# Cross-attention's last key block read in 64-row instead of 32-row TensorE tiles, with its values stored twice between zeros

## The chip, the cores and the metric

The kernel runs on one core of one Trainium2 chip. The metric is the device time of one execution in microseconds (us), lower is better. The time of the kernel before is the median of three runs.

## The reference

One transformer block in float32, batch 2, 1024 tokens of width 256, 16 heads of width 64: self-attention, cross-attention to a context of 154 tokens of width 192, and a gated feed-forward, each behind a layer norm and each added to its input. The part that matters here is cross-attention:

```python
def _attention(xq, xkv, wq, wk, wv, wo, bo):
    B, S, _ = xq.shape
    T = xkv.shape[1]                       # 154 context tokens
    q = (xq @ wq).reshape(B, S, N_HEADS, D_HEAD)
    k = (xkv @ wk).reshape(B, T, N_HEADS, D_HEAD)
    v = (xkv @ wv).reshape(B, T, N_HEADS, D_HEAD)
    attn = jnp.einsum('bihd,bjhd->bhij', q, k) * D_HEAD ** (-0.5)
    attn = jax.nn.softmax(attn, axis=-1)
    out = jnp.einsum('bhij,bjhd->bihd', attn, v).reshape(B, S, D_ATTN)
    return out @ wo + bo
...
x = _attention(h, cond_emb, ca_wq, ca_wk, ca_wv, ca_wo, ca_bo) + x
```

The change is in the second einsum: the softmax weights times the values of the context.

## The kernel before

Attention works on units: one batch element and one pair of heads, 16 units in all (`units`, `NU`). The whole program is emitted in one order written out by hand: a loop over the self-attention steps `p` (128 of them), then a loop over the cross-attention steps `c` (48, three per unit), then a loop over 64 feed-forward slots `k`, the first of which also hold the last steps of cross-attention. Every engine runs its instructions in that order. `run_work` slips projections, output projections and layer norms of other units between the steps; they lie in the lists `work`, `held`, `side` and `outs`. What a piece leaves to copy out is put on a list of stores and flushed a little later. `later` holds DMA issues, which are given out one or two a step.

In cross-attention step `c`, TensorE makes the scores (`sc`, L653), VectorE takes the row maxima (`neg`, L658), ScalarE the exponentials (L669), VectorE the reciprocals of their sums (L677), GpSimd scales the weights (L680), and VectorE transposes them in blocks of 32 by 32 (L696). After this, the 154 keys stand as five blocks of 32 (`NB`, the last one padded with zeros), with a key on each partition. Each of the four partition quarters `a4` (32 partitions each, `KB`) holds one quarter of the queries of a tile, so each quarter is multiplied separately.

So that the multiplication uses more than 32 rows of the array at once, `cross_regroup` moves the first four key blocks by DMA (`wf<-pT_ca` in the profile, since the target shares the buffer `wf`): two key blocks of a quarter are put one below the other, giving 64 rows (`QG`), in `pTc["pairs"]`. The fifth block (`NB - 1`) is not moved: it is read where the transpose left it, in the ring `pTc["ring"]`, as 32 rows of quarter `a4`.

`cross_values(ui, a2)` (L729) is the multiplication. It runs twice for each unit (`a2` of 0 and 1), 32 times in all. A call takes two quarters (`a2` and `2 + a2`) and two heads, so four products, and does each over `m` of 0, 1 and 2: two pairs of blocks, then the last block. The four products of one `m` use different parts of the array, and the profile shows them starting within a few nanoseconds of each other; each float32 matmul of the program appears as two records, so one call is 24 records. In the rest of the text a group of four records that start together is called a wave: a call is six waves, two for each `m`.

The values `v` are made by `values()`, once per two units (8 times): `pv` is projected from the context (L617), ScalarE copies it to `v` (L626, L627), and DMAs put copies where the other quarters need them. `v` lies in the pool `pt_` under the tag `V`, which has two buffers, shared with self-attention's values and, later, the feed-forward's products; a buffer is 8 KB per partition.

The first `values()` runs in the last self-attention steps (step 124), the second in cross step 5, the others every sixth cross step after (11, 17, and so on up to 41). From the third on, it follows the second `cross_values` call of a unit and the VectorE copies of its sums (`store` at L742).

Of the kernel before, what the change touches and what calls it, by code (L numbers as in the profile page):

```python
# [8 lines left out]
F32 = mybir.dt.float32  # L9
# [4 lines left out]
P = 128  # L14
# [4 lines left out]
def tile_transformer_block(ctx: ExitStack, tc: tile.TileContext, a: dict, out: bass.AP):  # L19
    nc = tc.nc  # L20
# [7 lines left out]
    DH = 64  # L28
# [8 lines left out]
    KB = 32  # L37
    NB = -(-T // KB)
    VC = 2 * P
    HB = 512  # L40
    QG = 2 * KB
    TP = NB * KB
    NM = P // QG
# [15 lines left out]
    pt_ = ctx.enter_context(tc.tile_pool(name="pt", bufs=2))  # L59
# [5 lines left out]
    def mm_tile(name):  # L65
        return ps_m.tile([P, HB], F32, tag="mm", name=name)

    def sum_tile(name):

        return ps_o.tile([P, HB], F32, tag="po", name=name)  # L70
# [19 lines left out]
    row_of, r = {}, 0  # L90
# [9 lines left out]
    for n in names[:2]:  # L100
        k = w[n].shape[0] // P
        nc.scalar.dma_start(
            out=cols[:, row_of[n]:row_of[n] + k], in_=w[n].rearrange("(r p) -> p r", p=P)
# [32 lines left out]
    for n in names[2:]:  # L136
        k = w[n].shape[0] // P
        nc.sync.dma_start(
            out=rows[row_of[n] - n_cols:row_of[n] - n_cols + k, :],
            in_=w[n].rearrange("(r p) -> r p", p=P),  # L140
# [34 lines left out]
    hT, vs, qk, oT = {}, {}, {}, {}  # L175
# [116 lines left out]
    def project_half(dst, name, wt, h, n, mul=None, parts=1):  # L292

        pq = mm_tile(f"p{name}_{n}")
        for i in range(parts):
            own = slice(i * HB // parts, (i + 1) * HB // parts)
            for c in range(NC):
                nc.tensor.matmul(  # L298
                    pq[:, own], lhsT=wt[:, c, :],
                    rhs=h[:, c, n * HB + own.start:n * HB + own.stop],  # L300
                    start=(c == 0), stop=(c == NC - 1),
                )
        if mul is None:

            dk = dst.rearrange("p (h n j) -> p n h j", h=2, j=KB)[:, n * NK // 2:(n + 1) * NK // 2]
            return lambda: nc.scalar.copy(dk, pq.rearrange("p (n h j) -> p n h j", h=2, j=KB))
        return lambda: nc.scalar.activation(dst[:, n * HB:(n + 1) * HB], pq, AF.Copy, scale=mul)
# [283 lines left out]
    def cross_pieces(b, pr):  # L591

        t = {}

        def q(n):
            if n == 0:
                t["q"] = p2.tile([P, S], F32, tag="QT", name=f"q_ca{b}_{pr}")
                t["k"] = p2.tile([P, S], F32, tag="KT", name=f"k_ca{b}_{pr}")
                qk["ca", b, pr] = (t["q"], t["k"])
            return project_half(t["q"], f"q_ca{b}_{pr}", wsl["ca", pr, "q"], hT["ca", b], n, scale)  # L600

        def keys():
            pk = mm_tile(f"pk_ca{b}_{pr}")
            for c in range(2):
                nc.tensor.matmul(
                    pk[:, :T], lhsT=wsl["ca", pr, "k"][:, c, :],
                    rhs=ctxT[:, c, b * TP:b * TP + T], start=(c == 0), stop=(c == 1),
                )
            return lambda: nc.scalar.copy(t["k"][:, :T], pk[:, :T])

        def values():

            v = vs["ca", b, pr // 2] = pt_.tile([P, NM + 1, VC], F32, tag="V", name=f"v_ca{b}_{pr}")
            pv = mm_tile(f"pv_ca{b}_{pr}")
            for n, rows_ in ((0, P), (1, KB)):
                for c in range(2):
                    nc.tensor.matmul(  # L617
                        pv[:rows_, n * VC:(n + 1) * VC],
                        lhsT=ctxT[:, c, b * TP + n * P:b * TP + n * P + rows_],
                        rhs=wsl["ca", pr, "v"][:, c, :], start=(c == 0), stop=(c == 1),  # L620
                    )

            def store():
                for n in range(NM):
                    own = slice(n * QG, (n + 1) * QG)
                    nc.scalar.copy(v[own, n, :], pv[own, :VC])  # L626
                nc.scalar.copy(v[:KB, NM, :], pv[:KB, VC:])  # L627
                later.insert(0, lambda: [
                    nc.sync.dma_start(
                        out=v[(1 - n) * QG:(2 - n) * QG, n, :], in_=v[n * QG:(n + 1) * QG, n, :])  # L630
                    for n in range(NM)
                ])
                later.insert(1, lambda: [
                    nc.sync.dma_start(out=v[a4 * KB:(a4 + 1) * KB, NM, :], in_=v[:KB, NM, :])
                    for a4 in range(1, P // KB)
                ])

            return store

        return [lambda: q(0), lambda: q(1), keys] + ([values] if pr % 2 == 0 else [])  # L640
# [74 lines left out]

    def cross_values(ui, a2):

        b, pr = units[ui]
        v, v0 = vs["ca", b, pr // 2], pr % 2 * P
        if a2 == 0 and pr % HP == 0:  # L720
            oT["ca", b, pr // HP] = pt_.tile([P, HP, S], F32, tag="oT", name=f"o_ca{b}_{pr}")
        quarters = (a2, 2 + a2)
        po = {a4: sum_tile(f"poc_{ui}_{a4}") for a4 in quarters}
        for m in range(NM + 1):
            for a4 in quarters:
                r0, n = (a4 // 2 * QG, QG) if m < NM else (a4 * KB, KB)
                r = slice(r0, r0 + n)
                for j in range(2):
                    nc.tensor.matmul(  # L729
                        po[a4][j * DH:(j + 1) * DH, :NT * KB],  # L730
                        lhsT=v[r, m, v0 + j * DH:v0 + (j + 1) * DH],
                        rhs=pTc["pairs"][r, a2, m, j] if m < NM else
                        pTc["ring"][r, ui % 3, NB - 1, j, :],
                        start=(m == 0), stop=(m == NM),
                        tile_position=(r0, j * DH),
                    )
        dst = oT["ca", b, pr // HP][:, pr % HP, :].rearrange(
            "p (t a q) -> p t a q", a=P // KB, q=KB)

        def store():  # L740
            for a4 in quarters:
                nc.vector.tensor_copy(  # L742
                    dst[:, :, a4, :], po[a4][:, :NT * KB].rearrange("p (t q) -> p t q", q=KB)
                )

        return store
# [24 lines left out]
    def cross_weigh(c):  # L771

        for part in range(2):
            ui, n = divmod(c - len(CG) - 4 - part, len(CG))
            if n == 0 and 0 <= ui < NU:
                run(lambda: cross_values(ui, part))
# [245 lines left out]
```

## Time and profile before

| what | value |
|---|---|
| median of 3 runs | 1167.21 us (1166.22 to 1169.26) |
| the profiled execution's own time | 1166.33 us |
| its span, first to last instruction | 1164.5 us |
| TensorE (PE) busy | 1141.3 us, 98% of the span |
| VectorE (DVE) busy | 828.9 us, 71% |
| GpSimd (POOL) busy | 665.8 us, 57% |
| ScalarE (ACT) busy | 643.3 us, 55% |
| cross-attention's value products (L729), span of time | 766.6 to 988.8 us |

Times are of one execution on the slowest core, which here is the only one. In a row such as `766.57 1.09 PE L729 MATMUL poc<-wf,v_ca 64*64 64x256 f32 x16` the first number is the start in us from the span's begin, the second the length, then come engine, line and operation, what is written and read, the tile of the array that is used (rows*columns), the streamed operand, and how many records were merged into the row. A time in brackets is idle time ahead of it, with what ended it. Ends of matmuls are modelled, so spacings are best read from starts.

Busy time by stretches of the span:

| stretch, us | PE | DVE | ACT | POOL |
|---|---|---|---|---|
| 710 to 740 (30) | 26.71 | 25.91 | 18.32 | 25.25 |
| 740 to 766 (26) | 26.00 | 8.63 | 12.43 | 8.19 |
| 766 to 960 (194) | 192.78 | 119.80 | 117.34 | 96.06 |
| 960 to 990 (30) | 30.00 | 12.91 | 7.19 | 9.65 |
| 990 to 1164 (174) | 170.67 | 42.21 | 35.16 | 9.06 |

### The profile page before, as it was taken

How to read it: one execution, taken by the hardware profiler on the slowest of the kernel's cores; microseconds unless marked ns; L12 is line 12 of the kernel's file. 1: busy time of each engine (PE TensorE's matmuls, PEld its weight loads, DVE VectorE, ACT ScalarE, POOL GpSimd, SP SyncE). 2: the span in 40 equal slices, each digit the busy share in tenths (PEclk: the TensorE clock that was granted, in tenths of full speed). 3: DMA queues.
4: the chain of work that ended last, by engine and by line, in shares of the span. 5: the costliest groups of instructions: out<-in, count | busy, mean ns of one | idle time of the engine just before them, and what ended most of it. 6: DMA issues, size and time to landing. Idle time of an engine off the chain costs nothing.

```text
span 1164.5 us, 31710 instructions
## 1 busy us (share of the span) xinstructions
PE 1141.3 (98%) x11931; PEld 673.2 (58%) x11931; DVE 828.9 (71%) x1170; ACT 643.3 (55%) x2055; POOL 665.8 (57%) x1556
## 2 busy tenths in 40 slices
PE   8999999999999999999999999899999999999998
PEld 5434444545545545545545455565566567888887
DVE  4888998898889889888999899557555664232222
ACT  5666676666666656656666666538655572041111
POOL 1778777876777777677777788626644453030000
PEclk9999999999999999999999999899999999999999
DMA  2311011111101101101111010167444433000000
GB/s 80 98 41 34 12 26 34 21 21 34 21 16 35 21 17 26 26 19 21 25 26 21 18 29 11 42 159 183 115 104 99 99 82 69 7 13 10 19 10 18
DMA packets 87234, 51.21 MB, mean 44 GB/s; under 512 B 30814, under 2 KB 77866, under 8 KB 87082
## 3 DMA queue, kind: packets, MB, share of 16 engines
q1 hardware_dynamic: 83866, 46.57, 17.5%
q10 hardware_dynamic: 3216, 2.62, 0.7%
q8 instruction: 94, 1.54, 0.6%
q14 instruction: 58, 0.48, 0.1%
HBM read 19.52 MB, written 2.10 MB: 19 GB/s over the span
## 4 chain that ended last, share of the span: by engine, by line
PE 82%; ACT 6%; POOL 3%; DVE 3%; DMA 2%; issue 2%; SPq 1%; DVEq 0%; ACTq 0%; POOLq 0%
PE po L428 16%; PE s L381 16%; PE pa L817 10%; PE py_sa L359 5%; PE py_ca L359 5%; PE pq_ca L298 5%; PE pf L840 5%; PE poc L729 4%; ACT p L392 4%; PE pv_sa L314 4%; PE pk_sa L298 3%; PE sc L653 3%; PE pq_sa L298 3%; DMA st<-st 2%; DVE st L541 2%
## 5 line engine op out<-in xcount | busy, mean ns | idle before, releaser
L392 ACT ACTIVATE p<-s,st 128x512 f32<-128x512 f32 x512 | 344.7, 685 | 217.9 <-DVE st L541 206.3
L492 POOL TENSOR_SCALAR p<-p,rd,ee 128x512 f32<-128x512 f32 x512 | 385.6, 767 | 43.7 <-DVE rd L488 42.7
L541 DVE TENSOR_REDUCE st<-s 128x2 f32<-128x1024 f32 x256 | 301.2, 1218 | 43.1 <-PE s L381 34.7
L506 DVE STREAM_TRANSPOSE pT<-p 128x1024 f32<-128x1024 f32 x256 | 302.3, 1218 | 1.7 <-POOL p L492 1.7
L381 PE MATMUL s<-k_sa,q_sa 64*32 64x512 f32 x4096 | 253.4, 596 | 12.5 <-ACT p L392 11.2
L428 PE MATMUL po<-pT,v_sa 64*64 64x256 f32 x4096 | 235.8, 379 | 0.0
L428 PEld LDWEIGHTS po<-pT,v_sa 64*64 64x64 f32 x4096 | 150.4, 133 | 109.1 <-issue 37.0
L680 POOL TENSOR_SCALAR p<-p,rden 128x154 f32<-128x154 f32 x256 | 96.8, 398 | 118.3 <-DVE rden L677 118.1
L669 ACT ACTIVATE p<-sc,neg 128x154 f32<-128x154 f32 x256 | 95.8, 394 | 86.6 <-DVE rden L677 82.9
L381 PEld LDWEIGHTS s<-k_sa,q_sa 64*32 64x32 f32 x4096 | 60.0, 105 | 142.4 <-issue 54.5
L817 PE MATMUL pa<-hT_ln,wf 128*128 128x256 f32 x512 | 121.0, 379 | 0.0
L826 DVE SCALAR_TENSOR_TENSOR u<-pa,cols,gate 128x256 f32<-128x256 f32 x64 | 30.9, 484 | 124.2 <-ACT gate L823 124.2
L823 ACT ACTIVATE gate<-pa,cols 128x256 f32<-128x256 f32 x64 | 30.3, 473 | 152.2 <-PE pa L817 152.2
L817 PEld LDWEIGHTS pa<-hT_ln,wf 128*128 128x128 f32 x512 | 96.8, 190 | 13.7 <-issue 0.8
L392 ACT ACTIVATION_READ_ACCUMULATOR p<-s,st 128x1 f32 x512 | 103.7, 202 | 0.0
L658 DVE TENSOR_REDUCE neg<-sc 128x6 f32<-128x924 f32 (+1 forms) x48 | 48.4, 1009 | 51.1 <-PE sc L653 51.1
L416 POOL TENSOR_TENSOR zz<-ee,st 128x8 f32<-128x8 f32 x128 | 25.9, 202 | 76.8 <-ACT ee L414 76.8
L314 PEld LDWEIGHTS pv_sa<-sa_wv,hT_ln 128*128 128x128 f32 x512 | 59.3, 192 | 16.3 <-issue 13.8
L840 PE MATMUL pf<-wf,u 128*128 128x256 f32 x256 | 65.0, 379 | 0.2 <-DVE u L826 0.2
L298 PE MATMUL pq_ca<-hT_ln,ca_wq 128*128 128x512 f32 x128 | 61.9, 625 | 0.5 <-ACT hT_ln L240 0.5
L314 PE MATMUL pv_sa<-sa_wv,hT_ln 128*128 128x128 f32 x512 | 62.4, 278 | 0.0
L359 PE MATMUL py_ca<-ca_wo,o_ca 128*128 128x256 f32 x256 | 60.8, 384 | 0.3 <-ACT hT_ln L240 0.3
(73 smaller groups left out, 1229.4 us busy)
## 6 DMA issues: line engine op xcount, KB each, us to landing
wf<-pT_ca SPq DMA_DIRECT2D x128, 128.0 KB, 2.4
st<-st SPq DMA_DIRECT2D x512, 1.0 KB, 1.7
v_sa<-v_sa SPq DMA_DIRECT2D x64, 128.0 KB, 2.5
wf<-in_L_xattn_ff_w_dram SPq DMA_DIRECT2D x12, 256.0 KB, 5.8
sa_wq<-in_L_xattn_sa_wq_dram SPq DMA_DIRECT2D x16, 128.0 KB, 2.3
sa_wk<-in_L_xattn_sa_wk_dram SPq DMA_DIRECT2D x16, 128.0 KB, 2.4
sa_wv<-in_L_xattn_sa_wv_dram SPq DMA_DIRECT2D x16, 128.0 KB, 2.4
ca_wq<-in_L_xattn_ca_wq_dram SPq DMA_DIRECT2D x16, 128.0 KB, 2.5
```

The costliest lines, as they stand in the source:

```text
L298: nc.tensor.matmul(pq[:, own], lhsT=wt[:, c, :], rhs=h[:, c, n * HB + own.start:n * HB + own.stop], start=(c == 0), stop=(c == NC - 1),)
L314: nc.tensor.matmul(pv[:, i * P:(i + 1) * P], lhsT=h[:, c, (n * GT + i) * P:(n * GT + i + 1) * P], rhs=wt[:, c, :], start=(c == 0), stop=(c ...
L359: nc.tensor.matmul(py[:, :D], lhsT=o[:, i, t * P:(t + 1) * P], rhs=wo[kind][:, half * HP + i, :], start=(i == 0), stop=(i == HP - 1),)
L381: nc.tensor.matmul(sc[a4 * KB:(a4 + 1) * KB, j, :], lhsT=q[r, c:c + KB], rhs=k[r, h * HB:(h + 1) * HB], start=True, stop=True, tile_positi ...
L392: nc.scalar.activation(pr[:, j, :], sc[:, j, :], AF.Exp, bias=st[:, 0, 0, i, j:j + 1], accum_out=st[:, 0, 1, i, j:j + 1],)
L428: nc.tensor.matmul(po[a2][j * DH:(j + 1) * DH, :QH // 2], lhsT=v[r, t, e, j * DH:(j + 1) * DH], rhs=pT[r, j * NK + n, :], start=(t == 0 an ...
L492: nc.gpsimd.tensor_scalar(pr[:, j, :], pr[:, j, :], rd[:, c:c + 1], ee[:, 0, c:c + 1], op0=ALU.mult, op1=ALU.mult,)
L506: nc.vector.transpose(halves[h][:, :, c:c + KB], groups.pop(0).rearrange("p j (n k) -> p (j n) k", k=KB))
L541: nc.vector.tensor_reduce(st[:, 0, 0, i, :], sc[i], AX.X, ALU.max, negate=True)
L680: nc.gpsimd.tensor_scalar(pr_[:, j, i, :T], pr_[:, j, i, :T], rden[:, j, i:i + 1], 1.0, op0=ALU.mult, op1=ALU.mult,)
L817: nc.tensor.matmul(pa[:, half, :TF * P], lhsT=w1[:, c, half * DF + f * P:half * DF + (f + 1) * P], rhs=h[:, c, t0 * P:(t0 + TF) * P], star ...
L840: nc.tensor.matmul(sums[blk][i][:, :D], lhsT=sums[blk, "u"][:, f, i * P:(i + 1) * P], rhs=w2[:, f, :], start=(f == 0), stop=(f == NF - 1),)
```

## The change

The values of the last key block get two slots of `v` instead of one, slots `NM` and `NM + 1`. Both are set to zero on VectorE when `v` is allocated. Slot `NM` gets the values in quarters 0 and 2, slot `NM + 1` in quarters 1 and 3; the other quarters stay zero. A matmul for quarter `a4` then reads all 64 rows of the half that `a4` lies in, from slot `NM + a2`, and streams the same 64 rows of the ring: the neighbouring quarter's weights meet zeros. The number of matmuls, their columns and the DMAs stay as they were; one of the three DMAs that copy the last block goes to slot `NM` and two to slot `NM + 1`.

```diff
         def values():
...
-            v = vs["ca", b, pr // 2] = pt_.tile([P, NM + 1, VC], F32, tag="V", name=f"v_ca{b}_{pr}")
+            v = vs["ca", b, pr // 2] = pt_.tile([P, NM + 2, VC], F32, tag="V", name=f"v_ca{b}_{pr}")
+            nc.vector.memset(v[:, NM:, :], 0.0)
...
                 later.insert(1, lambda: [
-                    nc.sync.dma_start(out=v[a4 * KB:(a4 + 1) * KB, NM, :], in_=v[:KB, NM, :])
+                    nc.sync.dma_start(out=v[a4 * KB:(a4 + 1) * KB, NM + a4 % 2, :], in_=v[:KB, NM, :])
                     for a4 in range(1, P // KB)
                 ])
...
         for m in range(NM + 1):
             for a4 in quarters:
-                r0, n = (a4 // 2 * QG, QG) if m < NM else (a4 * KB, KB)
-                r = slice(r0, r0 + n)
+                r0 = a4 // 2 * QG
+                r = slice(r0, r0 + QG)
                 for j in range(2):
                     nc.tensor.matmul(
                         po[a4][j * DH:(j + 1) * DH, :NT * KB],
-                        lhsT=v[r, m, v0 + j * DH:v0 + (j + 1) * DH],
+                        lhsT=v[r, m + a2 * (m == NM), v0 + j * DH:v0 + (j + 1) * DH],
                         rhs=pTc["pairs"][r, a2, m, j] if m < NM else
                         pTc["ring"][r, ui % 3, NB - 1, j, :],
                         start=(m == 0), stop=(m == NM),
                         tile_position=(r0, j * DH),
```

## The prediction

> **What bounds the kernel now.** I read the page's first part (busy time by engine), then the chain of waits that ended last, then who made TensorE wait in the stage that the change touches, and then the timeline of TensorE around one call of `cross_values`.
>
> ```profile
> PE 1141.3 (98%) x11931; PEld 673.2 (58%) x11931; DVE 828.9 (71%) x1170; ACT 643.3 (55%) x2055; POOL 665.8 (57%) x1556
> ...
> PE 82%; ACT 6%; POOL 3%; DVE 3%; DMA 2%; issue 2%; SPq 1%; DVEq 0%; ACTq 0%; POOLq 0%
> ```
>
> TensorE is busy for 98% of the span and holds 82% of the chain. That is an average, so the stage decides. The list of waits of TensorE from 766 to 992 us, the stretch that holds every L729 matmul, has three entries in all:
>
> ```profile
> PE pq_ca L298 <- ACT hT_ln L240: 0.5, 1, 0.5
> PE ph_ln L227 <- ACT hT_ln L240: 0.4, 1, 0.4
> PE py_ca L359 <- ACT hT_ln L240: 0.3, 1, 0.3
> ```
>
> That is 1.2 us of idle in 226, and the same list from 992 us to the end has one wait of 0.2 us. So from the first L729 matmul to the end TensorE is the bound, and what TensorE saves there moves the end.
>
> Now the call itself, in TensorE's timeline:
>
> ```profile
> 766.57 1.09 PE L729 MATMUL poc<-wf,v_ca 64*64 64x256 f32 x16
> 767.59 0.66 PE L729 MATMUL poc<-pT_ca,v_ca 32*64 32x256 f32 x8
> 768.18 0.79 PE L605 MATMUL pk_ca<-ctxT,ca_wk 96*128 96x154 f32 x4
> ```
>
> From start to start, four waves in 64-row tiles take 1.02 us and the two waves in 32-row tiles 0.59 us: 0.255 against 0.295 us for a wave of the same 256 columns. Self-attention gives a longer run of the same tile shape and columns:
>
> ```profile
> 716.65 3.69 PE L428 MATMUL po<-pT,v_sa 64*64 64x256 f32 x64
> 720.27 1.95 PE L381 MATMUL s<-k_sa,q_sa 64*32 64x512 f32 x32
> ```
>
> 64 records are 16 waves in 3.62 us. A straight line through the two 64-row runs has a slope of (3.62 - 1.02) / 12 = 0.217 us for a wave, and leaves 1.02 - 4 x 0.217 = 0.15 us for each run, whatever its length. The 32-row run obeys it too: 0.59 - 2 x 0.217 = 0.16. So a 32-row wave costs what a 64-row wave costs, and each run pays about 0.155 us once.
>
> Is the fixed cost paid for the change of tile shape, or for the change of the operands? The feed-forward changes operands and sums without changing the shape:
>
> ```profile
> 1040.24 1.89 PE L817 MATMUL pa<-hT_ln,wf 128*128 128x256 f32 x8
> 1041.96 1.03 PE L840 MATMUL pf<-wf,u 128*128 128x256 f32 x4
> 1042.83 1.46 PE L817 MATMUL pa<-hT_ln,wf 128*128 128x256 f32 x6
> ```
>
> Here 8 records take 1.72 us and 4 take 0.87, which is 0.215 and 0.2175 for a record: a change of operands alone costs nothing. I take the 0.155 us as the price of a change of shape.
>
> **What the Trainium skill says.** "TensorEngine Tiling (Array Packing)", section Key Properties: "Changing tiling mode (not just tile) drains the TensorE". The trace agrees, with 0.155 us a change. "VectorE: DVE Perf Modes", section Zero memsets can be issued as uint32 (trn2), says that a memset takes one cycle per element; its errata section gives VectorE 0.96 GHz and a fixed cost of 58 to about 150 cycles. No VectorE memset is in this trace. "SBUF — State Buffer", section Who interferes with whom, says that an instruction of VectorE with at most one SBUF input doesn't contend with GpSimd unless it runs in a two-port mode; no run here shows that yet.
>
> **The change part by part.**
>
> *Removed on TensorE: one change of shape per call.* The six waves of a call become one run. Now it is 1.02 + 0.59 = 1.61 us; then 6 x 0.217 + 0.155 = 1.457. Saving 0.155 us, times 32 calls: 5.0 us. The way out costs the same from 64 rows as from 32 (the L428 run above, which leaves for another shape, fits the same line). All 32 calls show this pattern, since the L729 groups hold 512 and 256 records with nearly constant durations. I see no gain below zero here: the number of matmuls, columns and weight loads is unchanged, and a 64-row weight load takes 133 ns against 130.
>
> *Added on VectorE: 8 memsets of 128 x 512.* Priced from the trace: statistics over 256 elements take 401 ns, a transpose of 1024 takes 1218, so 1.06 ns an element and 0.67 us for 512. The skill's cycles give an estimate of (512 + 58 to 150) / 0.96 = 0.59 to 0.69 us. I take 0.67; the low end, if it runs in a two-element mode, is 0.35, and the high end, if it has to wait out a GpSimd instruction of 0.77 us (L492) for a shared port, 1.45. In the order in which VectorE issues:
>
> - The first lies at step 124 between `rd` (711.17) and the reduction of the next scores (711.47). Self-attention runs closely there, VectorE being busy 25.91 of the 30 us from 710. But the next `rd` waits 0.53 us for GpSimd at 716.64, and that takes up most of the 0.67; left on the path is 0.1 us. At 1.45 us it would be 0.9, at 0.35 nothing.
>
> ```profile
> 711.47 2.35 DVE L541 TENSOR_REDUCE st<-s 128x2 f32<-128x1024 f32 x2
> 713.75 2.36 DVE L506 STREAM_TRANSPOSE pT<-p 128x1024 f32<-128x1024 f32 x2
> 716.64 0.18 DVE L488 RECIPROCAL rd<-den 128x4 f32<-128x4 f32 x1 [0.53 <-POOL den L418]
> ```
>
> - The second, at cross step 5, falls into a stretch in which VectorE is busy 8.63 of 26 us. Cost 0.
> - The other six stand behind the copies of a unit's sums (L742). What follows is waiting for TensorE anyway in most cases: after the copies at 874.75 VectorE is idle 2.92 us. In two cases (about 792 and 935 us) layer-norm statistics follow, and then the maxima of the next scores, idle 0.34 us at 793.50: they come 0.3 us late. Queued behind them are `rden` and the transposes; TensorE needs these products two steps later, some 10 us, so cost 0. If this cover were gone, each memset would cost its 0.67 us.
>
> *Waits.* The memset itself needs its buffer free of the last reader. The readers are the `cross_values` calls whose sums VectorE has just copied, so it waits for nothing new. ScalarE's copy of the last block now follows the memset, by a projection (L617) that TensorE runs later still. SP's queue has the same DMAs in the same order. The products need both slots only steps later. Cost 0.
>
> *Given back.* TensorE comes earlier to the three waits above, which hang on ScalarE's layer-norm copies. These come earlier too, as their inputs are from TensorE; only a call directly ahead of such a wait loses its 0.155. I allow 0.1 us.
>
> Sum: -5.0 + 0.1 + 0.1 = -4.8 us. The profiled execution goes from 1166.33 to 1161.5. The median of the runs stood 0.88 us above that execution, so the median goes from 1167.21 to 1162.4.
>
> **The rivals.**
>
> *A. The fixed cost stays.* What costs 0.155 us could be tied to the change of the streamed buffer to the ring or to fresh weights rather than to the tile's shape. For: shape and buffer always change together in L729. Against: the feed-forward rows, and the L428 run, which has new weights every wave at 0.217. Then only the memset's 0.1 is left: 1167.3.
>
> *B. Another engine takes over.* Once TensorE is 2% faster in this stage, a wait on ScalarE or on a regrouping DMA may eat half of it. For: the three waits. Against: VectorE, ScalarE and GpSimd are each busy under two thirds of 766 to 960. Half of 4.8: 1164.8.
>
> *C. The memsets cost more than the shape change saved: slower.* The place is VectorE's queue ahead of the score maxima; the mechanism is that memset and GpSimd's scaling lock each other out, so that a memset takes 1.45 us and the maxima, exponentials and next scores come late by all of it. It decides from 5.0 / 8 = 0.63 us exposed for each memset. At 1.45 us exposed: 8 x 1.45 - 5.0 = +6.6, so 1173.8. For: VectorE relays between TensorE, ScalarE and GpSimd. Against: the idle time after the copies.
>
> **How the numbers follow.** Forecast 0.70, A 0.10, B 0.12, C 0.08. About 0.3% (3.5 us) is what a measurement of this kernel can tell from no change. The forecast's own range is 1161.0 to 1163.7, from the spread of the runs before and a first memset between 0 and 0.9. Taking in B widens it to 1160.6 to 1165.4, which leaves out A and C, 0.18. Faster: the forecast and a little of B, 0.71; slower: C, 0.08; the same: 0.21.
>
> **What would show it.** Right: L729 becomes a single row of 24 records of 64*64 in TensorE's timeline, and from its start to the next line's is 1.45 us instead of 1.61; TensorE's busy time falls by about 5 us; eight VectorE memsets stand at about 0.67 us; TensorE's waits from 766 us on stay near 1.4 us. Wrong: the fifth and sixth waves keep their spacing (A); new waits of TensorE on ScalarE or DMA (B); memsets above 1 us, and scores that wait for the exponentials (C).

## The result and the profile after

The changed kernel is faster: 1163.6 us (median of 13 runs, 1160.26 to 1166.09) against 1167.11 us (13 runs, 1165.81 to 1169.28), a ratio of 0.9968 with a 95% interval of 0.9958 to 0.9978. By that ratio it is 3.7 us less (2.6 to 4.9); the medians differ by 3.5. The forecast was 4.8 less, so the direction and the range held and the size was too large by about 1.1 us. The spread within a kernel goes with TensorE's granted clock: the changed kernel's three runs at a mean of 0.998 or 0.999 took 1160.26 to 1161.41 us, its ten at 0.995 to 0.997 took 1163.01 to 1166.09.

First the call itself, in TensorE's timeline of the changed kernel (start, length, engine, line and operation, operands, tile, streamed operand, records):

```profile
769.89 1.09 PE L736 MATMUL poc<-wf,v_ca 64*64 64x256 f32 x16
770.80 0.61 PE L736 MATMUL poc<-pT_ca,v_ca 64*64 64x256 f32 x8
771.35 0.79 PE L605 MATMUL pk_ca<-ctxT,ca_wk 96*128 96x154 f32 x4
```

All 24 records are 64*64 now. From the call's start to the next line's it is 1.46 us; it was 1.61. The starts of the single records, which the timeline merges, give the six waves at distances of 267, 216, 216, 215 and 216 ns, with 326 to the next line; before they were 267, 216, 215, 326 and 267, with 324. Added up, a call is 0.16 us shorter, and this holds in nearly all of the 32 calls. On TensorE 5.1 us were saved, as forecast (5.0). The question is where 1.5 to 2 us of it went.

The waits of TensorE from 766 to 992 us (in total, times, longest) are longer than the 1.2 us of before:

```profile
PE pq_ca L298 <- ACT v_ca L631: 0.8, 1, 0.8
PE poc L736 <- DMA wf<-pT_ca: 0.5, 2, 0.3
PE ph_ln L227 <- ACT k_ca L609: 0.4, 1, 0.4
PE ph_ln L227 <- ACT hT_ln L240: 0.4, 1, 0.4
PE py_ca L359 <- ACT hT_ln L240: 0.3, 1, 0.3
```

They sum to 2.4 us, twice as much as before; in a second profile of the changed kernel, reported below, they sum to 3.0. So at least 1.2 us of the saving turned into waiting. One profile can't be compared with the other by its span alone: the profiled execution of the changed kernel has a span of 1164.3 us, against 1164.5, because it already lay 3 us behind at 130 us, where both programs do the same. Part of that is the granted clock: in the changed kernel's profile it is 0.50 for 3.4 us from 76.3 us on, where the profile of before has 1.00, and the lag grows by 1.6 us there, of which about half is made up again by 95 us. What can be compared is the course of the lag. I take the start of one and the same matmul in both profiles and subtract. The table gives that lag against the profile of before; a negative number is ahead of it. The last four columns are its change within a stretch; the stretches begin at starts of calls. The column for 766 us itself says nothing about the change: between 734 and 746 us each of the nine profiles has 3.4 or 6.8 us at a granted clock of 0.50 (before: 6.8 us from 735.7).

| kernel | lag at 766 us | 766 to 785 (2 calls) | 785 to 829 (7 calls) | 829 to 948 (16 calls) | 948 to 993 (7 calls) |
|---|---|---|---|---|---|
| full gain, 0.161 us a call | | -0.32 | -1.13 | -2.58 | -1.13 |
| changed | +3.32 | -0.32 | +0.12 | -2.55 | -0.78 |
| changed, run again | -0.31 | -0.31 | +0.11 | -2.55 | -0.79 |
| memsets only | -0.60 | 0.00 | +0.51 | 0.00 | 0.00 |
| memsets moved | +0.24 | -0.32 | -0.39 | -2.54 | -0.79 |
| later memsets on GpSimd | -2.02 | -0.32 | -0.45 | -2.54 | -0.86 |
| last block between the pairs | -1.84 | +0.33 | +0.53 | +2.58 | +0.80 |
| moved, and full projection | +0.23 | -0.32 | -0.60 | -3.79 | -0.79 |
| the same, norm later | -0.41 | -0.32 | -2.04 | -1.07 | -0.79 |

In the last row TensorE's work stands in another order from 800 to 872 us, so its two middle entries can only be read as a sum, -3.11, against -4.39 in the row above it.

Two stretches give all that was forecast. The one from 785 to 829 gives nothing at all: 1.25 us are missing. In the last one 0.34 us are missing, at the layer norm near 949 us, where TensorE's wait for `k_ca` grew from 0.10 to 0.42 us: a call lies right ahead of it.

What happens from 785 to 829? The chain starts on VectorE (changed kernel, VectorE's timeline):

```profile
794.33 0.72 DVE L749 COPY o_ca<-poc 128x256 f32<-128x256 f32 x2
795.11 0.48 DVE L617 MEMSET v_ca<- 128x512 f32 x1
795.51 0.37 DVE L196 BATCH_NORM_STATS2 st_ln<-x 128x6 f32<-128x256 f32 x1
...
796.54 0.13 DVE L212 SCALAR_TENSOR_TENSOR off_ln<-mv_ln,rstd_ln 128x2 f32<-128x2 f32 x1
```

goes on to ScalarE, in the same kernel's timeline of that engine,

```profile
796.70 1.09 ACT L218 ACTIVATE xn_ln<-x,off_ln,rstd_ln 128x256 f32<-128x256 f32 x2 [1.80 <-DVE off_ln L212]
797.70 0.74 ACT L630 COPY v_ca<-pv_ca 64x256 f32<-64x256 f32 x2
798.47 0.36 ACT L631 COPY v_ca<-pv_ca 32x256 f32<-32x256 f32 x1
```

and ends on TensorE, in its timeline:

```profile
796.07 1.98 PE L298 MATMUL pq_ca<-hT_ln,ca_wq 128*128 128x512 f32 x4
798.88 0.70 PE L298 MATMUL pq_ca<-hT_ln,ca_wq 128*128 128x512 f32 x1 [0.83 <-ACT v_ca L631]
```

The third memset stands ahead of the layer norm's statistics. `off_ln` comes late by it, ScalarE waits 1.80 us for `off_ln` with the copies of `v_ca` queued behind, and the projection of the next queries can't have its PSUM buffer before those copies have emptied it. Before, in the timelines of VectorE, ScalarE and TensorE:

```profile
785.80 1.12 DVE L658 TENSOR_REDUCE neg<-sc 128x6 f32<-128x924 f32 x1 [0.57 <-PE sc L653]
...
793.03 0.13 DVE L212 SCALAR_TENSOR_TENSOR off_ln<-mv_ln,rstd_ln 128x2 f32<-128x2 f32 x1
793.19 1.09 ACT L218 ACTIVATE xn_ln<-x,off_ln,rstd_ln 128x256 f32<-128x256 f32 x2 [1.30 <-DVE off_ln L212]
793.38 3.97 PE L298 MATMUL pq_ca<-hT_ln,ca_wq 128*128 128x512 f32 x8
```

ScalarE waited 1.30 us. No wait of TensorE is listed, but the starts of the single records show one: the fifth follows the fourth by 596 ns and the sixth follows it by 533, where 429 and 429 would do (the run with the last block between the pairs has these), so 0.27 us of waiting was hidden there already. In the changed kernel the distances are 1423 and 533 ns. And VectorE works from 785.80 to 793.16 us without a listed wait, with `off_ln` at the end, so a TensorE that gets ahead within these 7.4 us doesn't bring `off_ln` forward.

### The profile page after: what moved, and what is told of

It is laid out like the page before. It is cut to its first block, busy times and chain, and to the rows that moved or that the text cites. A ratio compares the mean times of both kernels' runs of the same rounds, so it can differ in the third digit from the quotient of the medians.

```text
span 1164.3 us, 31720 instructions
## 1 busy us (share of the span) xinstructions
PE 1138.8 (98%) x11931; PEld 677.9 (58%) x11931; DVE 832.8 (72%) x1178; ACT 644.2 (55%) x2055; POOL 669.2 (57%) x1556
## 4 chain that ended last, share of the span: by engine, by line
PE 76%; ACT 7%; POOL 5%; DMA 4%; DVE 4%; issue 3%; SPq 1%; DVEq 0%; ACTq 0%; POOLq 0%
PE po L428 15%; PE s L381 14%; PE pa L824 10%; PE py_ca L359 5%; ACT p L392 5%; PE pf L847 5%; PE pq_ca L298 4%; PE py_sa L359 4%; PE poc L736 4%; PE pq_sa L298 3%; PE pk_sa L298 3%; PE sc L657 3%; PE pv_sa L314 3%; DMA st<-st 3%; POOL p L492 3%
```

## The experiments

**Memsets alone.** The kernel before, with the larger tile and the memsets, and the last block still in 32-row tiles:

```diff
-            v = vs["ca", b, pr // 2] = pt_.tile([P, NM + 1, VC], F32, tag="V", name=f"v_ca{b}_{pr}")
+            v = vs["ca", b, pr // 2] = pt_.tile([P, NM + 2, VC], F32, tag="V", name=f"v_ca{b}_{pr}")
+            nc.vector.memset(v[:, NM:, :], 0.0)
```

> The kernel before with the larger values tile and the eight VectorE memsets, but with the last block still in 32-row tiles. Theory (part of the gain is lost to the memsets, at the first and the third of them): 1.0 to 1.6 us slower than before, so about 1168.4, and in its trace a new wait of TensorE for ScalarE's copies of v_ca near 795 us. Rival (the memsets are covered, and what was lost is TensorE running into limits of other engines because it is faster): no more than 0.3 us slower than before, and TensorE's waits from 766 us on as before, 1.2 us.

Measured: 1167.15 us against 1166.42, a ratio of 1.0009 (1.0003 to 1.0016), 1.0 us slower (0.3 to 1.9; the medians differ by 0.7). TensorE's waits from 766 to 992 us, in total, times, longest:

```profile
PE pq_ca L298 <- ACT hT_ln L240: 0.7, 1, 0.7
PE pq_ca L298 <- ACT v_ca L628: 0.5, 1, 0.5
PE ph_ln L227 <- ACT hT_ln L240: 0.4, 1, 0.4
PE py_ca L359 <- ACT hT_ln L240: 0.3, 1, 0.3
```

The new wait for the copies of `v_ca` is there without any gain on TensorE, and the lag grows by 0.51 us between 785 and 829 us and nowhere else from 766 us on. So the third memset costs 0.5 us; the second and the last five cost nothing. At the first the lag grows from 0.60 at 705 us to 0.99 at 717, but 0.17 of that comes ahead of the memset, and a kernel without a memset shows such a step too (0.28, in the next run). What follows the memset is 0.22 us. The rival, memsets wholly covered, falls: the trace is plain, the times alone only just exclude its 0.3 us.

**The last block between the pairs.** One more change of tile shape for each call, the same matmuls on the same operands, from the kernel before:

```diff
-        for m in range(NM + 1):
+        for m in (0, NM, 1):
...
-                        start=(m == 0), stop=(m == NM),
+                        start=(m == 0), stop=(m == 1),
```

> The kernel before with the last block multiplied between the two pairs, so that each call goes 64-row, 32-row, 64-row tiles: same matmuls, same operands, one change of tile shape more for each of 32 calls. Theory (a change of shape costs about 0.16 us, whatever the operands): 32 x 0.16 = 5.1 us slower than before, about 1172.2. Rival (the cost belongs to the buffer that is streamed from, or to what follows the call): within 1.5 us of before, since the same buffers are read, in another order, although a change of buffer is added too; the spacing of waves in the trace tells.

Measured: 1169.65 us, a ratio of 1.0029 (1.0017 to 1.0040), 3.4 us slower (2.0 to 4.7), which misses the 5.1. TensorE's timeline:

```profile
764.73 0.66 PE L729 MATMUL poc<-wf,v_ca 64*64 64x256 f32 x8
765.33 0.66 PE L729 MATMUL poc<-pT_ca,v_ca 32*64 32x256 f32 x8
765.91 0.66 PE L729 MATMUL poc<-wf,v_ca 64*64 64x256 f32 x8
766.51 0.66 PE L605 MATMUL pk_ca<-ctxT,ca_wk 96*128 96x154 f32 x3
```

Three runs of two waves take 1.78 us, 0.161 more than before. The shape's price is as expected. In this order the streamed buffer changes once more as well, so this run alone doesn't separate the two; the changed kernel does, since it kept the change of buffer and lost the 0.16. But only 4.2 of the 5.1 us arrive at the end of the stage. The table shows where the rest stayed: 785 to 829 us took 0.53 instead of 1.13, and the last stretch 0.80 instead of 1.13. There TensorE had waited anyway, and a slower TensorE waits less: the 0.27 us hidden at the projection are gone. It is the changed kernel's loss, seen in a mirror. What the median lies below the 4.2 is within the interval.

**The memsets moved.** From the changed kernel: the first memset goes ahead of the reciprocal that waits for GpSimd, the others behind the pieces that `run_work` slips into the same step.

```diff
+            if p == SA - SH:
+                new_values(*units[0])
+                zero(*units[0])
             if late:
                 late()
...
             run_work(2, 1, n_sum=2 * (SH < c < 2 * NPAIR and c % len(CG) == 0))
+            flush(zeros)
```

`new_values` allocates the tile, `zero` makes the memset, and `values()` puts it on the list `zeros` instead of issuing it.

> The changed kernel with the memsets moved in VectorE's order: the first ahead of the reciprocal that waits 0.53 us for GpSimd anyway, the others behind the layer-norm pieces of the same step. Theory (first and third memset cost 0.4 and 0.5 to 1.1 us by what stands behind them): 0.9 to 1.5 us faster than the changed kernel, about 1162.4, and no wait of TensorE for the copies of v_ca near 795 us. Rival (TensorE is limited by others there, wherever the memset stands): as the changed kernel, about 1163.6.

Measured: 1162.54 us, a ratio of 0.9965 to before (0.9952 to 0.9979). The times can't tell it from the changed kernel's 0.9968. The trace can: from 785 to 829 us 0.39 us now arrive where +0.12 had, 0.5 us recovered, and the wait for `v_ca` falls from 0.8 to 0.3 us:

```profile
PE pq_ca L298 <- ACT hT_ln L240: 0.7, 1, 0.7
PE ph_ln L227 <- ACT k_ca L617: 0.7, 2, 0.4
PE ph_ln L227 <- ACT hT_ln L240: 0.4, 1, 0.4
PE pq_ca L298 <- ACT v_ca L638: 0.3, 1, 0.3
PE py_ca L359 <- ACT hT_ln L240: 0.3, 1, 0.3
```

The part of the theory that names the third memset holds; that the wait for `v_ca` would go altogether does not, and 0.74 us are still missing in that stretch. The first memset, in its new place, has no step of the lag behind it.

**The later memsets on GpSimd.** The run above, but with VectorE free of memsets from cross-attention on:

```diff
-        nc.vector.memset(vs["ca", b, pr // 2][:, NM:, :], 0.0)
+        (nc.gpsimd if b or pr else nc.vector).memset(vs["ca", b, pr // 2][:, NM:, :], 0.0)
```

> The changed kernel with the first memset ahead of the reciprocal and the other seven on GpSimd, so that VectorE has none of them from cross-attention on. What is open is the 0.75 us that TensorE still doesn't gain from 784 to 830 us (7 calls, 1.13 us saved in spacings, 0.39 arrived) with the memsets moved. Theory (in this stretch VectorE's and ScalarE's layer-norm chain is the bound, with or without a memset): still about 0.7 us lost there, total as with the memsets moved, about 4.1 us faster than before. Rival (the third memset ahead of the score maxima costs the rest): no more than 0.3 us lost there, total 4.6 us faster than before.

Measured: 1162.1 us, a ratio of 0.9964 (0.9951 to 0.9978); in the stretch, 0.45 us of 1.13 arrive. With no memset on VectorE there, 0.68 us are still lost. So the remainder is not the memset's.

**The layer norm begun one unit later.** From the run "moved, and full projection" below:

```diff
-        if ui == 3:
+        if ui == 4:
             norm_beside("ca", B - 1)
```

> The run with moved memsets and the full projection, and the layer norm of the second batch element's cross-attention begins one unit (three steps) later. Theory (the layer-norm chain is the bound in its own stretch): the waits of TensorE for hT_ln and v_ca near 795 to 808 us move with it by about 14 us or shrink, and the stretch 784 to 800 gives TensorE's full gain of 0.16 us a call; the total changes by less than 1 us either way against 1161.06. Rival (the stretch is bound by what the steps always hold): the waits stay near 795 to 808 us.

Measured: 1161.65 us, a ratio of 0.9964 (0.9952 to 0.9977). From 785 to 798 us, where both runs still have TensorE's work in the same order, TensorE now gains 0.70 us where the run it starts from gains nothing. That is more than its own saving, because the 0.27 us that the kernel before waited there are gone too. Then the norm's matmuls and some of the output projection come later than in the other runs; by 872 us both have done the same work, and the gain since 785 us is 0.58 us instead of 1.87. TensorE's list of waits from 766 to 992 us begins with:

```profile
PE pq_ca L298 <- ACT v_ca L638: 1.0, 1, 1.0
PE poc L743 <- DMA wf<-pT_ca: 0.8, 1, 0.8
PE py_ca L359 <- ACT hT_ln L240: 0.5, 2, 0.3
```

The wait for `v_ca` went along with the norm, from 795 to 818 us (further than the 14 us expected, to the next `values()`), and a wait for `hT_ln` now stands at 829 us instead of 808. So this part of the lost gain follows the layer norm. The norm pieces are a chain over VectorE, GpSimd, ScalarE and TensorE; while they run, TensorE's saving is not passed on in full, though its listed waits are short. The wait for the DMA is new and stands in the old place, at 801 us. The price of the move was larger than expected: the whole stage comes out 1.3 us worse, where less than 1 was foreseen.

**A projection without a change of shape.** If a change of shape costs anywhere, the projection of the last block (L617, 32 columns of weights after 128) pays too. From the run with moved memsets: 128 columns, keys 32 to 159, so that the block lies in the last quarter and is copied to the others from there.

```diff
-            for n, rows_ in ((0, P), (1, KB)):
+            for n, k0 in ((0, 0), (1, TP - P)):
...
-                        lhsT=ctxT[:, c, b * TP + n * P:b * TP + n * P + rows_],
+                        lhsT=ctxT[:, c, b * TP + k0:b * TP + k0 + P],
...
-                nc.scalar.copy(v[:KB, NM, :], pv[:KB, VC:])
+                nc.scalar.copy(v[P - KB:, NM + 1, :], pv[P - KB:, VC:])
```

> The run above, and the last block's values are projected with 128 columns of weights (keys 32 to 159) instead of 32, so that the projection L617 has no change of tile shape either; the block then lies in the last quarter and is copied from there. Theory (each change of shape costs, at any place): the two spacings of 309 ns and the one of 240 around the 32-column part become 216, 0.2 us for each of 8, 1.5 us faster than the run above, about 1160.9. Rival (loading 128 columns of weights instead of 32 takes the gain back): as the run above.

Measured: 1161.06 us, a ratio of 0.9954 to before (0.9941 to 0.9966), 5.4 us faster: the lowest median of all, though its interval overlaps with that of the moved memsets. From 829 to 948 us the lag changes by 3.79 us against 2.54 without it, for four projections, so 0.31 us for each; I had counted 0.2, without the slower second matmul after the change. From 766 us on the sum is 1.46 us. That this is the expected 1.5 is luck: I had counted eight projections, of which six lie in the stage, and the two of these in the stretch from 785 to 829 us bring only 0.21 us together. The wider weights took nothing back.

**The changed kernel again.**

> The changed kernel once more, for a second profile. Theory (the 3.1 us by which its profiled execution lay behind the one of before at 92 us, ahead of all changed code, are the chance of that execution): another lag at 130 us, and from 784 us on the same course as in the first profile, minus 3.5 us from 766 us to the end. Rival (the changed program starts later): again 3 us behind by 130 us.

Measured: 1162.78 us against 1165.91, a ratio of 0.9974 (0.9963 to 0.9984). The second profile has a lag of 1.1 us at 130 us instead of 3.0, -0.31 instead of +3.32 at 766, and from there -3.54 us to the end of the stage, as the first had -3.53. The early lag is the chance of one execution; what the change does comes back to 0.01 us.

## Why the prediction was right, and where its sum was off

- *TensorE bounds the stage; a call saves 0.155 us.* The saving is right: 0.161 us measured, 5.1 us in all. The bound is right but for two stretches with a layer norm, where even the kernel before had TensorE waiting: made slower by 0.161 us a call, it took up 0.9 us there. The straight line through runs of 16, 4 and 2 waves had the price of a change of shape to within 5%.
- *A change of operands costs nothing (against rival A).* Right: the last two waves still stream from the ring, and their distances are 215 and 216 ns. Rival A is out.
- *The memset takes 0.67 us.* Too high: each of the eight is 0.485 us. Even so it cost more than forecast, because it stood in the wrong place.
- *The first memset costs 0.1 us.* 0.2 us at its place: from the matmul ahead of it to the one behind it, the lag grows by 0.24, 0.20 and 0.22 us in the three profiles that have it there, and not at all in the four that have it ahead of the reciprocal. VectorE's own later wait for GpSimd did take up part of it (0.53 us before, 0.30 after). Whether the 0.2 us reach the end is open: in two of the three profiles they are made up again by 732 us.
- *The other six behind the copies cost nothing.* This step failed for the third memset. I had named the statistics behind it, and followed the maxima, which do have time. The offsets `off_ln`, between the two, I didn't follow: ScalarE waited for them, with the copies of `v_ca` queued behind and a PSUM buffer held by those. It cost 0.5 us. The other five were free.
- *Given back: 0.1 us.* This term was mis-sized most: 1.0 us. The layer norm from 785 to 829 us withholds 0.7, the one near 949 us 0.3. This is rival B in two short stretches, not in the whole stage. I had argued that ScalarE's layer-norm copies come earlier since their inputs are TensorE's. The timelines show that they hang on `off_ln`, at the end of 7.4 us of VectorE's work: with the memsets moved, TensorE enters the call at 788.7 us 0.24 us earlier than before, but ScalarE begins `xn_ln` only 0.07 us earlier. I had also taken the three listed waits, 1.2 us, for all there was; 0.27 us more were hidden in the starts.
- *Rival C.* Its mechanism, memset and GpSimd blocking each other, didn't appear: the duration of all eight is 485 ns, minimum and maximum alike.

With these terms the sum is -5.1 + 0.2 + 0.5 + 1.0 = -3.4 us, against 3.7 (2.6 to 4.9) and 3.0 (1.9 to 4.3) us less measured. The forecast's range held with some luck: it was wide enough for a memset that is cheaper than counted and two terms that are dearer.

## What to carry to other kernels

Where short runs of matmuls in different tile shapes follow each other, count the changes of shape and their price, even when the smaller tiles seem to fit the data better: padding with zeros to the neighbour's shape can be cheaper. Before the saving of the busiest engine is put down in full, look for the short stretches where it waits at all, in the starts of single instructions as well as in the list of waits: there another chain is the bound, and the saving turns into a longer wait. And an instruction added to a queue is priced by everything that stands behind it on that engine until the next idle time, small ones like `off_ln` included, since a third engine may be waiting for just these.

## What was unexpected about the hardware

- VectorE's memset of 128 x 512 float32 took 485 ns in all eight cases, and in the three places of the changed kernel where VectorE had no idle time behind it, the next instruction started 0.40 us after it. The Trainium skill, "VectorE: DVE Perf Modes", section Zero memsets can be issued as uint32 (trn2), says that a memset takes one cycle per element; with the clock of 0.96 GHz from the same page that would be 533 ns, as an estimate. The measurement decides. GpSimd did the same in 524 ns.
- A change of tile shape costs more than the one gap: after the distance of 326 ns, the next wave still starts after 267 ns instead of 216. At the 32-column projection it was 0.31 us for two changes.
- One and the same code can reach 130 us with lags from -0.2 to +3.0 us against another execution. In two of the nine profiles 3.4 us at a granted clock of 0.50, near 75 us, added 1.6 us of it. A single span is no measure of a few microseconds; the lag over a stretch repeated to 0.01 us in the two profiles of the changed kernel.
